# Weighted sums of two attention groups in a row, behind both groups' scores, in a fused convolution, scan, attention and expert kernel

## The chip, the cores and the metric

The kernel runs on one core of a Trainium2 chip. The metric is the device time of one execution in microseconds (us). Engines are called by the profile's names: PE (TensorE; PEld are its weight loads), DVE (VectorE), ACT (ScalarE), POOL (GpSimd), SP (SyncE, which issues almost all transfers).

## The reference, cut to what matters

For a batch of four images of 128 channels and 64 x 64 pixels, in float32:

```python
x = x + conv_layer(group_norm(x))      # layer 0: depthwise conv, norms, and a
                                       # state-space scan with 16 states per channel
t = to_tokens(x)                       # 4096 tokens of 128 channels per image
q, k, v = split(ln(t) @ W_qkv + b_qkv) # 4 heads of 32 channels
s = einsum('bhnd,bhmd->bhnm', q, k) / sqrt(128)
t = t + (softmax(s) @ v) @ W_proj + b_proj
p = softmax(ln(t) @ router_w)          # 8 experts, the best two weighted
t = t + sum over experts of p[e] * (ln(t) @ expert_w[e] + expert_b[e])
out = from_tokens(t)
```

The change touches the attention: scores, their exponential, and the sum of the values weighted by it. The softmax is not shifted by the row's maximum; each value tile has 32 columns of ones beside its 32 value columns, so that the weighted sum gives numerator and denominator together.

## The kernel before, in words

**Blocks and slots.** An image is cut into 8 blocks of 512 tokens. The scan of a block takes 2 x 16 units (two channel halves, 16 states), and the attention of an image takes 256 groups: 4 pairs of query blocks (1024 queries) x 4 heads x 16 groups, where one group is STEP = 2 key tiles of 128 keys. One loop (L966 to L997) writes out the program for all of it, one slot after the other. A slot takes one scan unit (image b) and one attention group (image b-1, once the last block of that image is closed), so the attention of one image runs beside the scan of the next. There are 1024 units and 1024 groups; the first image's scan has no attention beside it, and the last image's attention has no scan beside it. "Shared stretch" below is the time in which a slot has both, "alone" the time in which it has the attention only.

**One slot, in order of emission:**
1. the scores of group s (`attention`, L761): two tiles `sc`, 128 keys x 1024 queries, two matmuls each with f32r operands (L785), and for each an exponential on ACT into `pT` (L790);
2. one stage of lane Y (convolution, norms, inputs of the scan);
3. `y`: an identity matmul that adds the last unit's product `hc` to the block's result;
4. one scan unit (`scan`, L644): `da` on ACT (L648), two broadcast transfers `bb` and `cc`, on DVE the product `h` (L660), the scan (L663) and `hc` (L670), and on ACT a copy of the last column to `state` (L668);
5. the weighted sums `av` of group s-1 (`weighted`, L796): four matmuls, each two instructions, with 64-column weights; two 64-column halves of the array work side by side;
6. one stage of lane X: `closed` (L683: projection, norm, and the queries, keys and values of a finished block, stored to DRAM), `divided` (L818: transpose and normalise a head's sums), `finished` (L827: output projection, norm, router, 8 expert stages, result). An expert stage is one `ps_X` matmul and four multiply-adds `acc` on DVE (L899).

**What fixes the order.** Every PE instruction passes through `queued` (L434), which ties it to the one before, so PE runs exactly the order of emission. On the other engines a scheduler places the instructions: `da`, the scan and its transfers are placed up to three units ahead, as their tiles have three buffers; exponentials follow their scores. SP issues in one order too: a store that waits for its data holds up the loads behind it, among them `ks` (keys, L774, one per four groups).

**Buffers.** The scores have two PSUM tiles (`ps_sc`, L461), which one group fills; the scores of the next group wait until ACT has read them. `pT` has four buffers, that is two groups. The sums `av`, the scan's result `y`, and the work tiles `ps_X` and `ps_Y` have one PSUM tile each; lane X's next matmul waits until DVE or ACT has read the last `ps_X`. After a head's 16 groups DVE copies `av` to `avs` (L809), and the head's `divided` stage, put at the front of lane X, transposes it.

Of the kernel before, what the change touches and what calls it, by code (L numbers as in the profile page):

```python
# [9 lines left out]
F32 = mybir.dt.float32  # L10
# [7 lines left out]
P = 128  # L18
C = 128
EPS = 1e-5  # L20
BLK = 512
NT = BLK // P
# [3 lines left out]
DH = 32  # L26
NH = 4
NE = 8
# [8 lines left out]
def conv_mamba_attn_moe_kernel(ctx: ExitStack, tc: tile.TileContext, t: dict):  # L37
    nc = tc.nc
    x, out = t["x"], t["out"]
    B, _, L = x.shape  # L40
# [68 lines left out]
    with (  # L109
# [20 lines left out]
        for i, (w, bias) in enumerate(((wqn, bqn), (wkn, bkn))):  # L130
            for h in range(NH):
# [9 lines left out]
                k = NH * i + h  # L141
# [318 lines left out]
    mix, att, side = pool("mix"), pool("att"), pool("side")  # L460
# [4 lines left out]
    def work(lane, shape=None):  # L465
        return ps_work.tile(shape or [P, BLK], F32, tag=f"work{lane}", name=f"ps_{lane}")

    def tmp(lane, name, shape=None):
        return side.tile(shape or [P, BLK], F32, tag=f"tmp{lane}", name=name, bufs=3)
# [206 lines left out]
        nc.gpsimd.tensor_mul(zs, xin, zs)  # L676
        gated[b, i, p] = zs

    vst = [side.tile([P, NH, NT, 2 * DH], F32, name=f"vst{k}") for k in range(2)]
    for w in vst:  # L680
        nc.gpsimd.memset(w[:, :, :, DH:], 1.0)

    def closed(b, i):  # L683

        if i == 0:
            kqv[b] = (
                dram.tile([2, P, L], F32, name="kd"), dram.tile([2, P, L], F32, name="qd"),
                dram.tile([NH, NB, P, NT * 2 * DH], F32, name="vd"),
                dram.tile([P, NTILE * C], F32, name="td"),
            )  # L690
        kd, qd, vd, td = kqv[b]
        s = slice(i * BLK, (i + 1) * BLK)
        ps = work("X")
        mm(ps.rearrange("p (r w) -> p r w", w=IMG), ident, y0_rows(b, i), True, False)
        mm(ps, skipI, xn_of[b, i][:, 3:], False, False)
        mm(ps, wout[:, 0, :], gated.pop((b, i, 0)), False, False)
        mm(ps, wout[:, 1, :], gated.pop((b, i, 1)), False, True)
        cm = tmp("X", "cm")
        nc.scalar.copy(cm, ps)
        yield  # L700
        xt = normalised("X", by_tile(transposed("X", by_tile(cm))))
        yield
        yield
        ps = transposed("X", xt)
        f = tmp("X", "f")
        nc.scalar.activation(f, ps, AF.Identity, bias=lnb, scale=lnw)
        xs = x_block(b, i, "xr")
        yield
        ps = work("X", [P, NT, C])
        for j in range(NT):  # L710
            r = slice(j * P, (j + 1) * P)
            summed(ps[:, j, :], [(f[:, r], projT), (xs[:, r], ident)])
        tt = side.tile([P, NT, C], F32, name="tt", bufs=2)
        nc.vector.tensor_add(tt, ps, projb[:, None, :].to_broadcast([P, NT, C]))
        nc.sync.dma_start(out=tsave[b][:, s], in_=tt.rearrange("p j c -> p (j c)"))
        xt = normalised("X", tt)

        nc.gpsimd.tensor_add(tt, tt, crow[:, None, :].to_broadcast([P, NT, C]))
        nc.sync.dma_start(out=td[:, s], in_=tt.rearrange("p j c -> p (j c)"))
        yield  # L720
        yield
        ps = transposed("X", xt)
        xa = side.tile([P, BLK], F32, name="xa", bufs=1)
        nc.scalar.copy(xa, ps)
        yield
        for d, w, bias in ((kd, wkn, bkn), (qd, wqn, bqn)):
            ps = work("X")
            mm(ps, w, xa)
            full = tmp("X", "full")
            nc.scalar.activation(full, ps, AF.Identity, bias=bias)  # L730
            hi = side.tile([P, BLK], F32R, name="hi")
            nc.scalar.activation(hi, ps, AF.Identity, bias=bias)
            lo = side.tile([P, BLK], F32R, name="lo")
            nc.vector.tensor_sub(lo, full, hi.bitcast(F32))
            nc.sync.dma_start(out=d[0][:, s], in_=hi.bitcast(F32))
            nc.sync.dma_start(out=d[1][:, s], in_=lo.bitcast(F32))
            yield
        ps = work("X", [P, NT, NH, DH])
        for j in range(NT):
            mm(ps[:, j].rearrange("p h d -> p (h d)"), xa[:, j * P : (j + 1) * P], wv)  # L740
        w = vst[i % 2]
        nc.vector.tensor_copy(w[:, :, :, 0:DH], ps.rearrange("p j h d -> p h j d"))
        nc.sync.dma_start(
            out=vd[:, i].rearrange("h p q -> p h q"), in_=w.rearrange("p h j d -> p h (j d)")
        )
        yield

# [48 lines left out]
    def weighted(group):  # L796
        b, qp, h, k0, pTs, ao = group
        if k0 == 0:
            sums[0] = ps_av.tile([P, BLK], F32, name="av")
        av = sums[0]  # L800
        for k, (v, pT) in enumerate(pTs):
            for u in range(2):
                mm(
                    av[64 * u : 64 * u + 2 * DH, :], v, pT[:, u, :],
                    k0 + k == 0, k0 + k == NTILE - 1,
                )
        if k0 + STEP == NTILE:
            avs = att.tile([P, BLK], F32, name="avs", bufs=2)
            nc.vector.tensor_copy(avs, av)  # L809
            lanes["X"].appendleft((("div", b, qp, h), divided(h, avs, ao), []))  # L810
            if h == NH - 1:
                for u in range(2):
                    qb = 2 * qp + u
                    lanes["X"].append(
                        (("out", b, qb), finished(b, qb, ao[:, u]), [("div", b, qp, h)])
                    )
# [10 lines left out]
    def finished(b, qb, ao):  # L827
# [5 lines left out]
        ps = transposed("X", ao.rearrange("p j h d -> p j (h d)"))  # L833
# [3 lines left out]
        ps = work("X", [P, NT, C])  # L837
# [4 lines left out]
        yield  # L842
        yield
        ps = transposed("X", xt)
        xf = side.tile([P, BLK], F32, name="xf")
        nc.scalar.copy(xf, ps)
        yield
        ps = work("X", [P, NT, NE])
# [41 lines left out]
        for j in range(NT):  # L890
            for u in range(2):
                ps = work("X", [P, NE // 2, C])
# [4 lines left out]
                for e in range(NE // 2):  # L897
                    k = NE // 2 * u + e
# [6 lines left out]
        ps = work("X")  # L905
        for j in range(NT):
            queued(nc.tensor.transpose(ps[0:NE, j * P : (j + 1) * P], pr[:, j, :], ident))
        prT = side.tile([NE, BLK], F32, name="prT")
        nc.scalar.copy(prT, ps[0:NE, :])
        yield  # L910
        ps = work("X")
# [9 lines left out]
    lanes, done, running = {"X": deque(), "Y": deque()}, set(), {}  # L921

    def advance(lane):

        while True:
            if lane not in running:
                if not lanes[lane] or not all(k in done for k in lanes[lane][0][2]):
                    return False
                running[lane] = lanes[lane].popleft()
            key, stages, _ = running[lane]  # L930
            try:
                next(stages)
                return True
            except StopIteration:
                done.add(key)
                del running[lane]
# [13 lines left out]
    for k in range(-2, len(blocks)):  # L950
        if 0 <= k:
            b, i = blocks[k]
            Y.append((("in", b, i, 1), inputs(b, i, 1), [("scan", *blocks[k - 1], 1)] if k else []))
        if k + 2 < len(blocks):
            b, i = blocks[k + 2]
# [3 lines left out]
        if 0 <= k + 1 < len(blocks):  # L959
            b, i = blocks[k + 1]  # L960
# [4 lines left out]
            ))  # L965

    units = iter([(b, i, p, n) for b, i in blocks for p in range(2) for n in range(NST)])
    term, waiting, groups, image = None, None, None, 0
    unit = next(units)
    while unit or term or waiting or image < B or lanes["X"] or running:  # L970
        if groups is None and image < B and ("closed", image, NB - 1) in done:
            groups = attention(image)
            image += 1
        group = next(groups, None) if groups is not None else None
        if groups is not None and group is None:
            groups = None
        advance("Y")
        if term:
            b, i, p, n, hc, y = term
            mm(y, ident, hc, n == 0, n == NST - 1)  # L980
            if n == NST - 1:
                scanned(b, i, p, y)
                done.add(("scan", b, i, p))
                if p == 1:
                    lanes["X"].appendleft((("closed", b, i), closed(b, i), []))
            term = None
        if unit:
            b, i, p, n = unit
            until(("in", b, i, p))
            if n == 0:  # L990
                y = ps_y.tile([P, BLK], F32, name="y")
            term = b, i, p, n, scan(b, i, p, n), y
            unit = next(units, None)
        if waiting:
            weighted(waiting)
        waiting = group
        advance("X")  # L997
    main.close()

    with tc.If(nc.values_load(general[0:1, 0:1]) > 0):
# [4 lines left out]
        with tc.For_i(0, B, 1) as b:  # L1007
            t_tok = whole.tile([P, NTILE, C], F32, name="t_tok")
            xa = whole.tile([P, L], F32, tag="xcm", name="xa")
            nc.sync.dma_start(  # L1010
                out=t_tok.rearrange("p k c -> p (k c)"),
                in_=tsave[bass.ds(b, 1)].rearrange("o p q -> (o p) q"),
            )
            with tc.tile_pool(name="ps_again", bufs=4, space=PSUM) as psum:
                for i in range(NB):
                    ps = anew(t_tok[:, NT * i : NT * (i + 1), :], psum)
# [86 lines left out]
```

## Time and profile before

| what | value |
|---|---|
| time, median of 3 runs | 6684.65 us (6683.0 to 6687.69) |
| profiled execution, its own time | 6685.48 us |
| its span, first to last instruction | 6683.4 us |
| mean granted PE clock | 0.924 |
| PE busy | 5909.8 us (88%) |
| DVE busy | 4012.6 us (60%) |
| ACT busy | 3703.8 us (55%) |
| `sc` matmuls | 4096 instructions, 1329.3 us |
| `av` matmuls | 8192 instructions, 2019.5 us |
| exponentials | 2048, 1020 ns each, 1985.6 us |
| first `sc`, last `y` | 1202.7 us, 5652.6 us |

The profiled execution took 0.8 us more than the median. Busy times of PE are modelled ends and overlap; start-to-start times of its instructions are exact. A bracket behind an instruction gives the idle time before it and what ended it. Four stretches are told apart below: before the first attention (to 1203 us), shared (to 5703 us), alone (to 6572 us) and the end.

### The profile page before, as it was taken

How to read it: one execution, taken by the hardware profiler on the slowest of the kernel's cores; microseconds unless marked ns; L12 is line 12 of the kernel's file. 1: busy time of each engine (PE TensorE's matmuls, PEld its weight loads, DVE VectorE, ACT ScalarE, POOL GpSimd, SP SyncE). 2: the span in 40 equal slices, each digit the busy share in tenths (PEclk: the TensorE clock that was granted, in tenths of full speed). 3: DMA queues.
4: the chain of work that ended last, by engine and by line, in shares of the span. 5: the costliest groups of instructions: out<-in, count | busy, mean ns of one | idle time of the engine just before them, and what ended most of it. 6: DMA issues, size and time to landing. Idle time of an engine off the chain costs nothing.

```text
span 6683.4 us, 69800 instructions
## 1 busy us (share of the span) xinstructions
PE 5909.8 (88%) x20282; PEld 2468.2 (37%) x20282; DVE 4012.6 (60%) x7806; ACT 3703.8 (55%) x5245; POOL 859.8 (13%) x895
## 2 busy tenths in 40 slices
PE   5777666899999898999989899999989899999996
PEld 2222222334344333434434343343434343444442
DVE  4788888666666575666757576666757575211122
ACT  2444434665565555566566565656556565555552
POOL 1212212111111111111111111111111110000000
PEclk7677767999999999999999999999999999999997
DMA  3454555555454654555555555445555455322220
GB/s 87 141 160 144 159 156 152 156 162 150 135 147 136 168 136 132 150 143 149 139 157 142 150 149 148 137 142 154 146 155 146 133 160 148 96 71 72 74 72 6
DMA packets 536343, 895.74 MB, mean 134 GB/s; under 512 B 100097, under 2 KB 183442, under 8 KB 535954
## 3 DMA queue, kind: packets, MB, share of 16 engines
q1 hardware_dynamic: 534786, 890.41, 47.0%
q8 instruction: 164, 2.69, 0.2%
q14 instruction: 225, 1.84, 0.1%
q10 hardware_dynamic: 1168, 0.80, 0.0%
HBM read 806.93 MB, written 83.89 MB: 133 GB/s over the span
## 4 chain that ended last, share of the span: by engine, by line
PE 54%; DVE 7%; DMA 3%; ACT 3%; issue 2%; POOL 1%; SPq 1%; DVEq 0%; ACTq 0%; POOLq 0%
PE av L444 21%; PE sc L444 11%; PE ps_X L444 9%; PE y L444 7%; PE ps_Y L444 4%; DMA bb<-bcd 2%; PE ps_X L474 1%; DVE h L663 1%; DVE xt L493 1%; DVE h L660 1%; DVE acc L899 1%; ACT pT L790 1%; DVE hc L670 1%; DMA ks<-kd 1%; PE ps_Y L474 1%
## 5 line engine op out<-in xcount | busy, mean ns | idle before, releaser
L790 ACT ACTIVATE pT<-sc 128x1024 f32<-128x1024 f32 x2048 | 1985.6, 1020 | 1033.1 <-PE sc L444 1031.1
L444 PE MATMUL av<-pT,v 128*64 128x512 f32 x8192 | 2019.5, 614 | 0.0
L444 PE MATMUL y<-hc,ident 128*128 128x512 f32 x2048 | 1244.8, 694 | 283.4 <-DVE hc L670 281.4
L444 PE MATMUL sc<-qs,ks 128*128 128x512 f32 x4096 | 1329.3, 446 | 123.0 <-DMA ks<-kd 55.4
L663 DVE TENSOR_TENSOR_SCAN h<-da,state,h 128x512 f32<-128x512 f32 x896 | 1194.0, 1333 | 58.3 <-DVE h L660 2.3
L444 PEld LDWEIGHTS av<-pT,v 128*64 128x64 f32 x8192 | 504.9, 138 | 1312.9 <-issue 1256.6
L444 PEld LDWEIGHTS sc<-qs,ks 128*128 128x128 f32 x4096 | 724.5, 191 | 659.7 <-issue 331.4
L660 DVE TENSOR_TENSOR h<-bb,du 128x512 f32<-128x512 f32 x1024 | 731.7, 715 | 373.5 <-DMA bb<-bcd 359.0
L648 ACT ACTIVATE da<-delta,amat 128x512 f32<-128x512 f32 x1024 | 738.5, 723 | 159.4 <-DVE h L663 150.5
L670 DVE TENSOR_TENSOR hc<-cc,h 128x512 f32<-128x512 f32 x1024 | 753.7, 737 | 90.7 <-DMA cc<-bcd 33.6
L668 ACT COPY state<-h 128x1 f32<-128x1 f32 x896 | 171.4, 192 | 993.3 <-DVE h L663 990.9
L444 PEld LDWEIGHTS y<-hc,ident 128*128 128x128 f32 x2048 | 396.7, 213 | 663.9 <-DVE hc L670 479.4
L899 DVE SCALAR_TENSOR_TENSOR acc<-ps_X,pr,acc 128x128 f32<-128x128 f32 x1024 | 356.1, 348 | 382.7 <-PE ps_X L444 361.5
L444 PE MATMUL ps_X<-w_ew,xf 128*128 128x512 f32 x512 | 302.2, 673 | 46.1 <-DVE acc L899 45.4
L809 DVE COPY avs<-av 128x512 f32<-128x512 f32 x64 | 44.1, 689 | 453.6 <-PE av L444 453.5
L489 POOL TENSOR_SCALAR rsX<-mvX 128x4 f32<-128x4 f32 x96 | 42.2, 440 | 1932.9 <-DVE mvX L487 1932.9
L444 PE MATMUL ps_Y<-y,taps 128*128 128x512 f32 x576 | 281.3, 627 | 3.7 <-ACT y L554 1.7
L444 PE MATMUL ps_Y<-xn,inxc 64*128 64x512 f32 x512 | 249.0, 628 | 2.5 <-DVE delta L630 1.6
L634 POOL TENSOR_TENSOR lost<-e,lost 128x512 f32<-128x512 f32 x64 | 99.7, 1558 | 1099.7 <-DVE lost L633 1091.8
L493 DVE TENSOR_SCALAR xt<-ps_Y,mvY,rsY 128x128 f32<-128x128 f32 x384 | 132.3, 404 | 171.4 <-POOL rsY L490 171.4
L489 POOL TENSOR_SCALAR rsY<-mvY 128x4 f32<-128x4 f32 x96 | 44.0, 458 | 1294.4 <-DVE mvY L487 1292.0
L676 POOL TENSOR_TENSOR zs<-xin,zs 128x512 f32<-128x512 f32 x64 | 106.2, 1660 | 722.6 <-DVE xin L675 722.5
(207 smaller groups left out, 4613.9 us busy)
## 6 DMA issues: line engine op xcount, KB each, us to landing
bb<-bcd SPq DMA_DIRECT2D x2048, 128.0 KB, 3.4
cc<-bcd SPq DMA_DIRECT2D x2048, 128.0 KB, 3.5
ks<-kd SPq DMA_DIRECT2D x1024, 128.0 KB, 3.4
v<-vd SPq DMA_DIRECT2D x256, 256.0 KB, 3.9
qs<-qd SPq DMA_DIRECT2D x256, 128.0 KB, 3.4
vd<-vst SPq DMA_DIRECT2D x32, 512.0 KB, 3.2
xg<-in_x SPq DMA_DIRECT2D x32, 256.0 KB, 4.1
gn<-in_x SPq DMA_DIRECT2D x32, 256.0 KB, 3.9
```

What stands on the lines that cost most here:

```text
L444: queued(nc.tensor.matmul(out, lhsT=lhsT, rhs=rhs, start=start, stop=stop))
L474: queued(nc.tensor.transpose(ps[:, j * P : (j + 1) * P], src[:, j, :], ident))
L493: nc.vector.tensor_scalar(xt[:, j, :], src[:, j, :], mv[:, j, 0:1], rs[:, j : j + 1], ALU.subtract, ALU.mult)
L634: nc.gpsimd.tensor_sub(lost, e, lost)
L648: nc.scalar.activation(da, delta, AF.Exp, scale=amat[:, n : n + 1])
L660: nc.vector.tensor_mul(h, bb, du)
L663: nc.vector.tensor_tensor_scan(out=h, data0=da, data1=h, initial=0.0 if i == 0 else state[:, p, n : n + 1], op0=ALU.mult, op1=ALU.add,)
L668: nc.scalar.copy(state[:, p, n : n + 1], h[:, BLK - 1 : BLK])
L670: nc.vector.tensor_mul(hc, cc, h)
L676: nc.gpsimd.tensor_mul(zs, xin, zs)
L790: nc.scalar.activation(pT, sc, AF.Exp, scale=ATT_SCALE)
L899: nc.vector.scalar_tensor_tensor(acc[:, j, :], ps[:, e, :], pr[:, j, k : k + 1], acc[:, j, :], ALU.mult, ALU.add,)
```

## The change

The loop no longer takes the weighted sums of group s-1 in slot s. It collects two groups, and when both have their scores, it writes out the weighted sums of both in a row, behind lane X's stage. Over two slots PE's order was

    sc0 Y y av X | sc1 Y y av X

and becomes

    sc0 Y y X | sc1 Y y X av0 av1

The groups' number per head (16) is even, so a pair never spans two heads. Beside that, five tiles lose buffers or move to the shared `tmpX` ring of three: `vst` (2 buffers to 1), `tt` (2 to 1), `xa`, `xf`, `prT`. The PSUM pools and the buffers of `pT`, `ks` and `v` stay.

```diff
-    vst = [side.tile([P, NH, NT, 2 * DH], F32, name=f"vst{k}") for k in range(2)]
-    for w in vst:
-        nc.gpsimd.memset(w[:, :, :, DH:], 1.0)
+    vst = side.tile([P, NH, NT, 2 * DH], F32, name="vst")
+    nc.gpsimd.memset(vst[:, :, :, DH:], 1.0)
...
-        tt = side.tile([P, NT, C], F32, name="tt", bufs=2)
+        tt = side.tile([P, NT, C], F32, name="tt")
...
-        xa = side.tile([P, BLK], F32, name="xa", bufs=1)
+        xa = tmp("X", "xa")
...
-        xf = side.tile([P, BLK], F32, name="xf")
+        xf = tmp("X", "xf")
...
-        prT = side.tile([NE, BLK], F32, name="prT")
+        prT = tmp("X", "prT")[0:NE, :]
...
-    term, waiting, groups, image = None, None, None, 0
+    term, waiting, groups, image = None, [], None, 0
...
-        if waiting:
-            weighted(waiting)
-        waiting = group
         advance("X")
+        if group:
+            waiting.append(group)
+
+        if len(waiting) == 2 or (waiting and group is None):
+            for group in waiting:
+                weighted(group)
+            waiting = []
```

More of the change, by code (lines that the diff above doesn't have):

```diff
@@ L740, in closed @@
             mm(ps[:, j].rearrange("p h d -> p (h d)"), xa[:, j * P : (j + 1) * P], wv)
-        w = vst[i % 2]
-        nc.vector.tensor_copy(w[:, :, :, 0:DH], ps.rearrange("p j h d -> p h j d"))
+        nc.vector.tensor_copy(vst[:, :, :, 0:DH], ps.rearrange("p j h d -> p h j d"))
         nc.sync.dma_start(
-            out=vd[:, i].rearrange("h p q -> p h q"), in_=w.rearrange("p h j d -> p h (j d)")
+            out=vd[:, i].rearrange("h p q -> p h q"), in_=vst.rearrange("p h j d -> p h (j d)")
         )
@@ L967, in conv_mamba_attn_moe_kernel @@
     units = iter([(b, i, p, n) for b, i in blocks for p in range(2) for n in range(NST)])
-    term, waiting, groups, image = None, None, None, 0
+    term, waiting, groups, image = None, [], None, 0
     unit = next(units)
-    while unit or term or waiting or image < B or lanes["X"] or running:
+    while unit or term or waiting or groups or image < B or lanes["X"] or running:
         if groups is None and image < B and ("closed", image, NB - 1) in done:
```

## The prediction

> **What bounds the kernel now.** I read the busy time by stretch first, then the waits of the shared stretch, then PE's instructions in order of time, then the waits that remain. By stretch (columns: stretch, length, then PE, PEld, DVE, ACT, POOL busy with instruction counts, granted clock, DMA share, GB/s):
>
> ```profile
> 1203.00:5703.00 4500.00, 4169.06 (x14937) 1775.33 (x14937) 2889.97 (x5538) 2720.93 (x3866) 601.62 (x615) 0.97 0.53 147
> 5703.00:6572.00 869.00, 862.21 (x3548) 357.25 (x3547) 164.91 (x583) 511.78 (x550) 10.11 (x16) 1.00 0.24 69
> ```
>
> PE sets the pace: 93% busy in the shared stretch, 99% alone. But busy PE is not useful PE. PE's own timeline, four plain slots (start, length, instructions):
>
> ```profile
> 3010.73 1.20 PE L444 MATMUL sc<-qs,ks 128*128 128x512 f32 x4
> 3011.76 1.02 PE L444 MATMUL y<-hc,ident 128*128 128x512 f32 x2
> 3012.71 1.94 PE L444 MATMUL av<-pT,v 128*64 128x512 f32 x8
> 3014.58 1.20 PE L444 MATMUL sc<-qs,ks 128*128 128x512 f32 x4
> ```
>
> A slot is 3.85 us. In the single records two `y` instructions are 0.429 apart, an `av` instruction costs 0.2145 on average, an `sc` one 0.235. From these, `y` to `av` should take 0.86 and takes 0.95 (+0.09); eight `av` should take 1.72 and take 1.87 (+0.15); `sc` to `y` should take 0.94 and takes 1.04 (+0.10). So entering and leaving an `av` run costs **0.34 us**, in every slot.
>
> What waits are there in the shared stretch (waiting instruction, released by, us in total, times, longest):
>
> ```profile
> PE y L444 <- DVE hc L670: 91.5, 37, 5.2
> PE sc L444 <- DMA ks<-kd: 55.4, 17, 8.3
> PE ps_X L474 <- DVE avs L809: 52.2, 28, 3.6
> PE sc L444 <- ACT pT L790: 7.9, 21, 1.5
> ```
>
> The last line matters most: today scores hardly wait for the exponentials, because 1.87 us of `av` lie between one group's scores and the next. The change takes that cover out of every first half of a pair.
>
> **The change part by part.** All sums stand against the profiled execution, 6685.5 us, 0.8 above the median.
>
> *Fewer runs of `av`.* The order of PE's instructions in the changed program has 512 `av` runs instead of 1024. Alone: 128 runs less, charted below. Shared: 384 x 0.346 = 133, times 0.93 (the share in which PE is the pace; elsewhere another wait takes the gain over) = **-124**. A rule of the Trainium skill speaks against this: "TensorE: Matmul & The Clock Gate", Part 2, step-by-step, has PE pull weight loads ahead of matmuls in flight. By it the border would be nearly free and my sum some 168 us higher. Here the first weight load of `av` is not pulled ahead: it starts at 3012.71, with its matmul, 0.76 us after the load before it.
>
> *Head's end.* `divided` ran right behind the last `av` and waited for the copy `avs` (0.69 us). Now scores and `y` (1.04 + 0.86) lie between. Gone: the 52.2 above x 0.93 = **-48**; alone, 59.4 on the page less 52.2 = -7.
>
> *Lane X ahead of `av`.* X1 now runs before two `av` runs instead of directly before the next scores, so what hangs on X1 has 3.7 us more. The case where this pays, on PE and SP:
>
> ```profile
> 2583.67 1.12 PE L444 MATMUL ps_X<-xa,w_wqn 128*128 128x512 f32 x2
> 2590.82 2.04 PE L444 MATMUL sc<-qs,ks 128*128 128x512 f32 x4 [6.03 <-DMA ks<-kd]
> 2592.66 1.91 PE L444 MATMUL y<-hc,ident 128*128 128x512 f32 x2
> ```
>
> ```profile
> 2586.12 0.34 SPq L735 DMA_DIRECT2D qd<-hi  x1
> 2586.85 0.34 SPq L736 DMA_DIRECT2D qd<-lo  x1
> 2587.24 0.45 SPq L756 DMA_DIRECT2D ks<-kd  x1
> ```
>
> SP's queue is held by the store of the queries, which waits for X1's matmul, ACT and DVE; the keys behind it land 7.1 us after X1 begins. Charted with the new order from sc0 (2575.37) at 0, with the durations around it: X0 at 1.80, sc1 2.66 to 3.60, X1 at 4.46; ACT does sc1's exponentials to 6.3, then X1's two copies to 7.7, DVE the third to 8.4, the store is out at 8.8, the keys land 3.5 later (2587.24 to 2590.73). sc2 starts at 12.35 instead of 15.45: 3.1 less, 2.8 beyond the border. Twelve such waits of 5 to 6.3 us: -33. Twenty-one other waits ahead of an even group's scores could save 34 (each up to 2.07); half of it, 17. Together **-50**. The skill's clock rule (same page, Part 1: half speed after an idle window of 3.4 us) would add 12 x 1.7 = 20, as the wait falls to about 3 us. Not counted: `y` runs at half speed after the 6.03 wait (1.91 for 1.02), but at 2569.03 a wait of 2.92 was followed by `av` at 3.68 for 1.94 too.
>
> *Shared stretch, the price.* From sc0 to sc1 the distance shrinks by 1.87 of `av` plus 0.20 of border: 2.07. For every second slot I took from the single records how long before its start each PE stage had its inputs and buffers ready, and charged what 2.07 exceeds that by, the largest once per slot. In 214 to 229 of 384 slots something is late: scores behind exponentials 42, expert matmuls behind `acc` 43 (`ps_X` is one buffer), other stages of X and Y 63, `y` behind `hc` 103. Of the last, 26 slots wait newly (25 us); 35 wait already (77 us), mostly for `bb` behind a store held by X one slot earlier, which now comes sooner. They could as well gain 72. I take none of it: 42 + 43 + 63 + 25 = **+173**; bounds for `y` alone -72 to +103.
>
> *Alone.* No `y`, no Y, and lane X only sometimes. The slots now (PE and ACT):
>
> ```profile
> 5895.85 1.20 PE L444 MATMUL sc<-qs,ks 128*128 128x512 f32 x4
> 5896.68 1.94 ACT L790 ACTIVATE pT<-sc 128x1024 f32<-128x1024 f32 x2 [1.06 <-PE sc L444]
> 5896.98 1.94 PE L444 MATMUL av<-pT,v 128*64 128x512 f32 x8
> 5898.84 1.20 PE L444 MATMUL sc<-qs,ks 128*128 128x512 f32 x4
> ```
>
> 2.99 a slot, 5.99 a pair. New pair, from sc0 at 0: exponentials start at 0.83, end at 1.80 and 2.77; a score can follow 0.05 later (smallest distance in the records). PE reaches sc1 at 1.04, waits to 1.85 for the first tile and to 2.82 for the second, ends at 3.29; then 0.14 entry, 16 x 0.2145 = 3.43, 0.09 exit: 6.95, so +0.96. With an expert stage in both slots (3.86 each now): sc1's second tile still waits to 2.82; X1 waits for X0's multiply-adds, which end 2.67 after its matmul begins at 1.04 (now 5804.68 to 5807.35), so until 3.76; the pair ends at 8.28 for 7.72: +0.56. In the changed order's 128 pairs, between sc0 and sc1 stand: nothing in 57 (55 us), four transposes of 0.59 in 25 (same end 6.95 for 6.58: 9), a matmul of 0.86 in 38 (32 expert pairs 18, six at +0.1), others in 8. Sum 83, less 7 for the heads' ends: **+76**, borders included.
>
> *Free.* `vst`, `tt`, `xa`, `xf`, `prT`: each is next written many slots after its last reader (blocks come 32 slots apart, and in lane X's program order no ring tile comes round before its reader is done). If that cover failed, a DVE or ACT write would wait about one landing per block, 32 x 3.2 us (`vd<-vst` on the page) = 102. The sums and exponentials themselves are unchanged; `av1` needs an exponential that ends at 4.71 in the chart and is read at 5.15.
>
> Sum: -124 - 48 - 50 + 173 + 76 = +27: 6685.5 + 27 = **6712 us**.
>
> **Rivals.** (1) *Lane X's early start wins (faster)*: the held stores on SP go out 2 to 4 us sooner, so `bb`, `h` and `hc` come sooner too. Place: the 35 slots in which `y` waits today. Price: -72, and if half of the other 148 is covered by waits already there, -74 more: 6712 - 146 = 6566 at best, about 6620 at half. It decides if the shared stretch falls by more than 76, what the lone stretch loses. For it: those waits stand at fixed places in each block behind stores. Against: ACT, DVE and `ps_X` serve one slot at a time, and half the slots lose 2.07 of slack.
>
> (2) *`y` pays in full*: +77, and the short `ks` waits give nothing, +17: 6806. Against it the same fixed places.
>
> (3) *The terms cancel* (within 0.2%, 13 us, about what this kernel's measurement can tell): 6685.
>
> (4) *It doesn't do what it says*: the border is paid between av0 and av1 as well; 168 + 27 gives 6880. Nothing in the records shows a cost between `av` instructions on different `pT`, so almost nothing for it.
>
> **How the numbers follow.** Forecast, a small loss (6699 to 6760) 0.37; rival 1 0.32; rival 2 0.17; rival 3 0.13; rival 4 0.01. Slower 0.37 + 0.17 + 0.01 = 0.55, same 0.13, faster 0.32. Range 6600 to 6800: it holds rival 1 down to a little below its half and nearly all of rival 2; the likeliest sign's own range is 6699 to 6760.
>
> **What would show it.** Alone grows from 869 to about 945, and idle time of the `sc` weight loads behind ACT there well beyond 104 us; shared shrinks by about 50; PE's wait for `avs` near 0; waits for `ks` down by some 30; waits for `acc` and `hc` up. The issue-idle of `av` weight loads (1256.6 us on the page) must halve; if not, rival 4. I am wrong if the lone stretch doesn't grow (PE would not wait for the exponentials), or if `y`'s waits move by more than 70 either way.

## The result, and the profile after

The changed kernel takes 6802.1 us (median of 4 runs, 6789.12 to 6810.56), against 6685.0 for the kernel before on the same chip: ratio 1.0173, 95% interval 1.0156 to 1.0191. It is slower, as forecast, but by 117 us and not by 27, and 2 us beyond the range. The profiled execution is the lowest of the four, 6789.12 us with a span of 6787.2, so the stretches below add up to 104 and not to 117.

First the stretches of the changed kernel, shared and alone (columns as in the prediction: stretch, length, then PE, PEld, DVE, ACT, POOL busy with instruction counts, granted clock, DMA share, GB/s):

```profile
1201.00:5709.00 4508.00, 4115.75 (x14938) 1822.28 (x14939) 2906.28 (x5540) 2718.06 (x3866) 624.76 (x615) 0.97 0.54 147
5709.00:6674.00 965.00, 886.99 (x3543) 361.51 (x3541) 164.63 (x582) 505.45 (x550) 10.12 (x16) 1.00 0.22 62
```

From group to group in the records, the lone stretch grew from 868.8 to 965.7: **+97**. The shared stretch went from 4500.2 to 4507.5: **+7**, where I had expected -49. In the shared stretch PE's busy time fell by 53 and its idle time rose by 61; the second line shows PE idle for 78 of 965 us alone, where it had been idle for 7.

What the lone stretch now looks like, on PE and then on ACT (start, length, instructions, idle before and its releaser):

```profile
6002.00 1.10 PE L444 MATMUL ps_X<-w_ew,xf 128*128 128x512 f32 x2 [0.20 <-DVE acc L897]
6003.03 3.65 PE L444 MATMUL av<-pT,v 128*64 128x512 f32 x16
6006.61 1.20 PE L444 MATMUL sc<-qs,ks 128*128 128x512 f32 x4
6007.65 1.02 PE L444 MATMUL ps_X<-w_ew,xf 128*128 128x512 f32 x2
6008.52 0.73 PE L444 MATMUL sc<-qs,ks 128*128 128x512 f32 x2
6009.44 0.73 PE L444 MATMUL sc<-qs,ks 128*128 128x512 f32 x2 [0.18 <-ACT pT L788]
6010.36 0.60 PE L905 MATMUL ps_X<-ident,pr 128*8 128x128 f32 x4 [0.19 <-DVE acc L897]
```

```profile
6007.44 3.85 ACT L788 ACTIVATE pT<-sc 128x1024 f32<-128x1024 f32 x4 [4.52 <-PE sc L444]
```

The sixteen `av` run on in 3.65 us, eight pairs at 0.429 and the last one's own end: nothing is paid between the two groups. But the second group's scores are cut in two tiles of two, and the second waits. ACT says why: it works through four exponentials without a gap from 0.83 us after the first score, and has had 4.52 us of idleness before. Twice the scores and exponentials now fall together and then stand still together.

In the shared stretch, what PE waits for (us in total, times, longest):

```profile
PE y L444 <- DVE hc L670: 109.9, 50, 5.8
PE ps_X L444 <- DVE acc L897: 87.0, 45, 9.6
PE sc L444 <- ACT pT L788: 50.5, 124, 3.1
...
PE sc L444 <- DMA ks<-kd: 26.4, 10, 8.6
```

`avs` is down to 0.8 us and `ks` by 29, as worked out; `acc` (16.8 before), the exponentials (7.9) and `hc` took their place.

### The profile page after: what moved, and what is told of

Its sections match the earlier page's. It is cut to its first block, busy times and chain, and to the rows that moved or that the text cites. A ratio compares the mean times of both kernels' runs of the same rounds, so it can differ in the third digit from the quotient of the medians.

```text
span 6787.2 us, 69668 instructions
## 1 busy us (share of the span) xinstructions
PE 5878.5 (87%) x20282; PEld 2519.8 (37%) x20282; DVE 4028.5 (59%) x7806; ACT 3695.9 (54%) x5245; POOL 882.2 (13%) x894
## 5 line engine op out<-in xcount | busy, mean ns | idle before, releaser
L444 PE MATMUL av<-pT,v 128*64 128x512 f32 x8192 | 1913.9, 609 | 8.6 <-ACT pT L788 8.6
L444 PE MATMUL y<-hc,ident 128*128 128x512 f32 x2048 | 1222.9, 683 | 302.2 <-DVE hc L670 300.0
L444 PEld LDWEIGHTS sc<-qs,ks 128*128 128x128 f32 x4096 | 683.2, 189 | 951.3 <-issue 518.1
L444 PEld LDWEIGHTS av<-pT,v 128*64 128x64 f32 x8192 | 551.5, 139 | 1203.1 <-issue 1071.7
L444 PEld LDWEIGHTS ps_X<-w_ew,xf 128*128 128x128 f32 x512 | 93.8, 201 | 262.7 <-issue 175.9
```

Of the source, the lines that this page charges most:

```text
L444: queued(nc.tensor.matmul(out, lhsT=lhsT, rhs=rhs, start=start, stop=stop))
```

## The experiments

Theories, by the letters that the expectations use. **A**: the second group's scores wait for the first group's exponentials. **B**: lane X's stages follow too closely on `ps_X`, whose one buffer waits for the multiply-adds into `acc`. **C**: the shared stretch is paced by another chain (SP, transfers, the scan on DVE), so that what PE saves is taken back there, whichever wait shows it. **D**: the lost buffers cost. **Y**: `y` comes before its product `hc`. **S** (formed late): exponentials are late because they queue behind ACT's copy `state`, which waits for the scan.

Two measures are used. Ratios are against the kernel before on the same chip. Stretches come from one profile each, and profiles on different chips differ: e2 below has a ratio of 0.9998, and a shared stretch 14 us shorter than the first profile of before. So stretches on one chip are set against each other where that is to be had.

### Parts of the change alone

e1, one group at a time, lane X ahead of its weighted sum (against before):

```diff
+        advance("X")
         if waiting:
             weighted(waiting)
         waiting = group
-        advance("X")
```

> Only lane X's place changes: a slot is scores, Y, y, X, av of the group before; one group at a time, buffers as before. Theory A (the pair uncovers the second group's scores, and that alone spoils it): no pair, no uncovered scores; PE's wait for the copy of a head's sums (59 us before) goes to nearly 0 and part of the keys' waits (55 us) too, so 60 to 100 us faster, 6585 to 6625. Theory C (in the shared stretch a chain over SP, transfers and VectorE sets the end, and whatever PE gains there is taken back): shared stretch 4500 as before, 6675 to 6690.

Ratio 0.9828 (0.9815 to 0.9842), 6556.08 us: the fastest of the kernels here that do the whole work. Shared 4380.1, alone 865.5. The move of lane X, which the change brings along, is worth 1.7% by itself; the pairing loses it and more. What PE still waits for in e1's shared stretch:

```profile
PE y L444 <- DVE hc L670: 50.5, 29, 5.4
PE sc L444 <- DMA ks<-kd: 35.5, 13, 5.4
```

Before, these two were 91.5 and 55.4; the wait for `avs` is down from 52.2 to 4.9.

e2, the buffer edits alone (the first half of the change's diff, with before's loop):

> The five buffer edits alone (vst, tt, xa, xf, prT), with the loop of before. Theory A and C: no tile is written again before its readers are long done, 6678 to 6692. Theory D (the buffer edits are part of the loss): a wait of a few us per block, 30 to 100 us slower.

Ratio 0.9998 (0.9989 to 1.0007); shared 4486.4, alone 868.7. Theory D falls.

e3, pairs, but the second slot's lane X behind the two sums:

```diff
-        advance("X")
         if group:
             waiting.append(group)
...
             waiting = []
+        advance("X")
```

> The changed kernel with the second slot's lane X behind the two weighted sums instead of ahead of them. Theory A: the uncovered scores stay (110 us of wait in the shared stretch, 117 alone), the waits for the copy of the sums (about 60) and for the keys (about 55) come back: 6880 to 6920. Theory C: shared stretch as it is, about 6800.

6842.89 us in a single run, shared 4558.2, alone 972.5. Between the two groups' scores stands the same work as in the change; only the second stage of lane X has moved, from ahead of the two sums to directly ahead of the next scores. The shared stretch is 51 us longer than that of the change's pairs on the same chip (e4, below). PE's waits for `avs` are back at 23.2 us (0.8 in the changed kernel), those of `y` for `hc` are 132.3 (109.9).

e4, pairs only while scan terms run beside them, before's order alone:

```diff
+        if unit or term:
+            advance("X")
+            ...
+        else:
+            for old in waiting:
+                weighted(old)
+            waiting = [group] if group else []
+            advance("X")
```

> Pairs as long as the scan runs beside the attention, one group at a time (order of before) in the last image. Theory A: the lone stretch falls from 965 back to about 869, the shared one stays at about 4508: 6690 to 6715. Theory B (lane X's single work buffer is what the pair costs): only some 10 us of the lone stretch come back, about 6790.

Ratio 1.0024 (1.0015 to 1.0034): shared 4507.2, alone 868.8. So of the change's 1.73% the lone stretch holds about 1.5, all of it given back by the order alone. On this chip e1, e2 and e4 stand side by side: lane X ahead takes 4486 to 4380 (**-106**), and pairs on top of it take 4380 to 4507 (**+127**).

### One suspected wait taken away at a time

e5 (on e1) and e6 (on the changed kernel), exponentials cut short so that scores hardly wait for them:

```diff
-                        pT = att.tile([P, 2, BLK], F32, name="pT", bufs=4)
-                        nc.scalar.activation(pT, sc, AF.Exp, scale=ATT_SCALE)
+                        pT = pTf[turn[0] % 4]
+                        turn[0] += 1
+                        nc.scalar.activation(
+                            pT[:, :, 0:64], sc[:, :, 0:64], AF.Exp, scale=ATT_SCALE
+                        )
```

> Control: one group at a time, lane X ahead of av (the order of e1_x_first), and each exponential covers 128 of its 1024 columns (the other columns of pT keep ones written at the start), so the scores' buffers come free some 0.7 us sooner each. Theory A (the pair's loss is the second group's scores waiting for exponentials): scores hardly waited here, so the lone stretch stays at 866 and the shared one falls little, 4330 to 4380. Theory C (the shared stretch is set by SP, transfers and VectorE): the same.

> The changed kernel with the same short exponentials. Theory A: the second group's scores don't wait any more; the lone stretch falls from 965 to about 825 (866 less 128 x 0.34), the shared one from 4508 to below 4400. Theory B (what the pair costs in the shared stretch is lane X's single work buffer and the scan's products coming late): lone stretch the same 825 to 845, but the shared one still above 4430.

A single run each; an exponential covers 128 of its 1024 columns, and the other columns of `pT` keep ones. e5: 6524.98 us, shared 4347.0, alone 864.6. e6: 6606.29, shared 4427.3, alone 867.7. Alone, the stretch is 98 us shorter with the exponentials cut, which is as much as the pairs had lost. PE's timeline of e6 there:

```profile
5910.52 1.20 PE L444 MATMUL sc<-qs,ks 128*128 128x512 f32 x4
5911.56 0.60 PE L474 MATMUL ps_X<-ident,ao 128*128 128x128 f32 x4
5911.91 1.17 PE L444 MATMUL sc<-qs,ks 128*128 128x512 f32 x4
5912.92 1.07 PE L444 MATMUL ps_X<-w_wp,aT 128*128 128x128 f32 x8
5913.92 3.65 PE L444 MATMUL av<-pT,v 128*64 128x512 f32 x16
```

The second group's four scores run as one block, with nothing in brackets. A plain pair (no stage of lane X in it) falls from 7.07 to 5.88 us. Theory A is shown for the plain pairs. The 28 pairs with an expert stage in both slots don't move, 8.36 us with and without the cut, for there theory B holds as well; PE's longest wait in e6's lone stretch is the one for `acc`:

```profile
PE ps_X L444 <- DVE acc L905: 21.5, 28, 0.8
```

Such an expert pair takes 7.92 with one multiply-add alone (e7) and 7.35 with both cuts (e12). In the shared stretch the pair gains 80 and the single order 33.

e7, the changed kernel with one of four multiply-adds into `acc` per expert stage:

```diff
-                for e in range(NE // 2):
+                for e in range(1):
```

> The changed kernel with one multiply-add per expert stage instead of four (three of four experts' products are left out), so lane X's work buffer comes free about 1.0 us sooner. Theory B: PE's wait for it (98 us in the shared stretch) falls by most, the shared stretch from 4508 to 4420 or less. Theory A: 30 to 50 us, since scores wait on instead.

6697.4 us in a single run, shared 4460.0 (-47), alone 952.9 (-13). What PE waits for in its shared stretch:

```profile
PE y L444 <- DVE hc L670: 146.0, 68, 5.6
PE sc L444 <- ACT pT L788: 47.8, 115, 3.1
...
PE ps_X L444 <- DVE acc L897: 17.1, 11, 4.4
```

The wait for `acc` fell by 70 (87.0 to 17.1), and that for `hc` rose by 36. Half of what is taken away at one place comes back at the next.

e10 (on e1) and e11 (on the changed kernel), `y` one slot later:

```diff
-        if term:
-            b, i, p, n, hc, y = term
+        if len(terms) == 2 or (terms and not unit):
+            b, i, p, n, hc = terms.popleft()
...
+            terms.append((b, i, p, n, scan(b, i, p, n)))
```

> One group at a time, lane X ahead of av (e1_x_first, ratio 0.983, shared stretch 4380), and y takes the scan's product of two units ago instead of the last one. Theory Y (PE comes to y before the scan's product is there, 57 us of wait; a slot more of distance hides it): shared stretch 4320 to 4350, ratio 0.974 to 0.979. Theory C (the scan's chain over transfers and VectorE is itself behind at these places, so PE only waits later): 4370 to 4390, ratio 0.982 to 0.985.

> The changed kernel (pairs) with the same later y. Theory Y: PE's wait for the scan's product, 122 us there, falls below 40, the shared stretch from 4507 to 4400 to 4440. Theory C: the wait only moves to the next scores or lane stage, 4490 to 4510.

e10: ratio 0.9852 (0.9836 to 0.9869), no better than e1; shared 4361.3, but from a start some 34 us later, so the time did not follow. e11: 6769.63 in a single run, shared 4455.4 (-52), alone 965.7. Again the waits of e11 tell where the rest went:

```profile
PE ps_X L444 <- DVE acc L897: 102.4, 43, 8.0
PE sc L444 <- ACT pT L788: 71.9, 139, 3.3
PE sc L444 <- DMA ks<-kd: 39.9, 18, 5.4
```

`hc` has left the list (109.9 before the edit); `acc` has 15 more, the exponentials 21, the keys 14.

### All of them together

e12 (pairs) and e13 (the single order of e1): short exponentials, one multiply-add and the later `y`.

> The changed kernel with all three waits taken away at once: short exponentials (128 of 1024 columns, the rest of pT is ones), one multiply-add per expert stage instead of four, later y. If these three are what the pair costs, the saved border shows in full against e13: lone stretch 44 below it (about 820), shared stretch 90 to 130 below it. Theory C: lone stretch so, but the shared stretch no better than e13's, or above it.

> Control for e12: one group at a time, lane X ahead of av, with the same three cuts. Lone stretch 865; shared stretch 4280 to 4340 (4347 with short exponentials alone, less what the later y and the missing multiply-adds give).

A single run each: 6465.35 and 6465.17 us. e12: shared 4315.3, alone 835.3. e13: shared 4286.0, alone 864.6. Alone the pair is now ahead by 29, of the 44 (128 x 0.346) that its border is worth; an expert pair, with 7.35 us where the order before took 7.71, has it in full, a plain one, 5.88 for 5.99, only a third: even the short exponential (0.83 after the first score, then 0.28 long) ends after PE is back at the scores, which start 1.16 us after the first ones where 1.04 was possible. In the shared stretch the pair is still 29 behind, where its saved border should put it some 124 ahead. ACT's own waits in e12's shared stretch:

```profile
ACT state L668 <- DVE h L663: 962.6, 470, 6.5
ACT da L648 <- DVE h L663: 151.8, 72, 6.3
```

Of 54 second slots in which scores still waited (61 us), the exponentials were late in all, and in 39 of them ACT had stood before `state`. So theory S: `state` on ACT holds the exponentials up.

e14 (on e1), e15 (on the changed kernel), e16 and e17 (on e12 and e13) put that copy on DVE:

```diff
-            nc.scalar.copy(state[:, p, n : n + 1], h[:, BLK - 1 : BLK])
+            nc.vector.tensor_copy(state[:, p, n : n + 1], h[:, BLK - 1 : BLK])
```

> One group at a time, lane X ahead of av (e1_x_first: ratio 0.983, shared 4380), with the copy of the scan's last column on VectorE behind the scan instead of on ScalarE. Theory S (ScalarE stands before this copy until the scan is done, and exponentials behind it come late): few scores are late here, so 10 to 40 us less in the shared stretch. Theory C (the scan's chain on VectorE and the transfers sets the stretch): 896 more VectorE instructions of about 0.1 to 0.2 us make it 0 to 100 us longer.

> The changed kernel (pairs, shared 4508, alone 965) with the same move. Theory S: the 54 late exponentials go, some 40 to 60 us less in the shared stretch; alone unchanged. Theory C: not shorter.

> Pairs with the three cuts of e12_all_pair (short exponentials, one multiply-add per expert stage, later y: shared 4315) and the copy on VectorE. Theory S: the border shows at last, shared stretch 50 to 130 below e17's. Theory C: the pair still isn't ahead of e17 by more than 20.

> Control for e16: single groups, lane X ahead, the same four cuts (e13_all_single without the copy's move: 4286). Theory S: 4260 to 4286. Theory C: 4290 to 4380.

e14: ratio 0.9852 (0.9835 to 0.9868), shared 4377.0. e15: 6794.54, shared 4506.7. e16: 6468.01, shared 4313.2. e17: 6474.63, shared 4289.7. Nothing moves by more than the profiles of two chips differ. The same wait of ACT in e16:

```profile
ACT da L648 <- DVE h L663: 1103.3, 526, 6.5
```

It has only gone from `state` to `da`, the next instruction, whose buffer the scan must free: 962.6 + 151.8 = 1114.4 before, 1103.3 now. Theory S falls. ACT's stream is tied to the scan on DVE at two places, and freeing one is worth nothing.

### Another spacing

e9, to give the pair its cover back: in each round of two slots all of lanes Y and X and both `y` are spread around the two groups' scores, and both sums are written at the end; the single order of e1 alone.

```diff
+            advance("X")
+        for _ in range(2 if beside else 1):
+            advance("Y")
             if term:
...
+            second = next(groups) if group else None
+            advance("X")
+            if group:
+                weighted(group)
+                weighted(second)
```

> Pairs whose second scores stand far from the first: beside the scan two slots are scores, X, Y, y, Y, y, scores, X, av, av; alone, one group at a time with lane X ahead of av. Theory A: scores find their buffers free (two y of 0.86 and a stage of X between), the border is saved 384 times, so 60 to 120 us faster than lane X's move alone: ratio 0.965 to 0.974. Theory C: nothing beyond lane X's move, ratio about 0.983; if two y in a row wait for the scan's products, above that.

Ratio 1.0207 (1.019 to 1.0224): shared 4603.4, alone 865.5. What theory A gave for it is missed by a wide margin. PE's waits in e9's shared stretch:

```profile
PE y L444 <- DVE hc L670: 190.7, 81, 5.8
PE av L444 <- ACT pT L788: 66.6, 50, 3.6
PE ps_X L444 <- DVE xt L493: 64.9, 15, 5.0
```

The scores' waits are gone from the head of the list; 81 us more of `y` and 58 more of `av` than in the changed kernel stand there. Two terms close together ask for two products in quick succession, where the change's order asks for one per slot.

### Where PE's time goes, kernel by kernel

In the records of single matmuls I added up the distances from each start to the next in the shared stretch, by what they lead to. The five sums make up the stretch exactly: *av* (into, within and out of `av`, up to the second scores instruction), *sc* (the other two scores), *y*, *X*, *Y*.

| kernel | av | sc | y | X | Y | shared |
|---|---|---|---|---|---|---|
| e1, single | 2113 | 374 | 601 | 807 | 485 | 4380 |
| e4, pairs (same chip) | 2034 | 411 | 674 | 884 | 505 | 4507 |
| changed kernel | 2029 | 413 | 673 | 885 | 508 | 4508 |
| e6, pairs, short exponentials | 1990 | 374 | 693 | 882 | 489 | 4427 |
| e7, pairs, one multiply-add | 2024 | 409 | 721 | 799 | 507 | 4460 |
| e11, pairs, later `y` | 2073 | 418 | 544 | 913 | 507 | 4455 |
| e12, pairs, all three | 2035 | 380 | 553 | 830 | 516 | 4315 |
| e13, single, all three | 2112 | 364 | 540 | 771 | 499 | 4286 |

e1 to e4 is the price of pairing term by term: -78 + 36 + 73 + 77 + 20, 127 as rounded sums go. And the rows below show C at work: e7 takes 86 off X and gives 48 back at `y`; e11 takes 129 off `y` and gives 28 back at X and 45 in the *av* sum, at the first scores.

These sums hold more than work and waiting: PE's clock differs too. The shared stretches of e1 and e4 (columns as above, the granted clock behind the counts of POOL):

```profile
1201.00:5581.00 4380.00, 4143.51 (x14937) 1789.22 (x14935) 2881.81 (x5540) 2723.73 (x3868) 628.80 (x615) 0.98 0.53 151
1198.00:5705.00 4507.00, 4128.30 (x14934) 1822.69 (x14935) 2911.14 (x5538) 2717.54 (x3866) 624.27 (x615) 0.97 0.51 147
```

In the records of these traces the granted clock is either 1 or 0.5. Pieces at 0.5 (3.4 us long or a multiple of that) add up to 292 us in e2's shared stretch, 164 in e1's and 301 in e4's. They follow idleness of PE: in the 3.5 us before a fall e4's PE has stood still for 2.3 us in the median, before any other moment for none. Half of PE's busy time in these pieces is my estimate of what they cost: 120 us in e2, 72 in e1, 126 in e4, and 49 in e13 against 91 in e12. By that estimate some 48 of the 106 that lane X's move gains, and some 54 of the 127 that pairs cost on top of it, are PE running slowly after a wait. No run changes the clock by itself, and the waits that follow would take a part of it back, so these shares are not shown by an experiment. The mean clock of the whole execution repeats: 0.933 to 0.935 in all five runs of e1, 0.923 to 0.928 in all ten of e4.

## Why the prediction was wrong

The sign was right, and the waits that the prediction names are those that appeared; the sum was 90 short of the median (6712 for 6802): 56 in the shared stretch (+7 for -49), 21 alone (+97 for +76), and 13 that the profiled execution lies below the median. To judge the shared stretch by the prediction's own terms I set each distance between two PE starts against a short one (the 5% point) between the same instructions at full clock, and put the rest down to what the second one had waited for. From e2 (before's order) to e4 (pairs), on one chip, in us:

| term of the shared stretch | predicted | e2 to e4 |
|---|---|---|
| fewer runs of `av` | -124 | -135 |
| head's end, `avs` | -48 | -50 |
| lane X ahead: keys and values ahead of scores | -50 | -65 |
| scores behind exponentials | 42 | 87 |
| their restart (the last section) | 0 | 16 |
| expert matmuls behind `acc` | 43 | 74 |
| other stages of X and Y | 63 | 48 |
| `y` behind `hc` | 25 | 27 |
| sums behind their own exponentials | 0 | 15 |
| half clock, other waits | 0 | 4 |
| sum | -49 | 21 |

Against the 25% point the first row comes to -147 and the restart to 24; no other row moves by more than 6. The first profiles of before and after give the same picture, with 95 for the scores, 74 for `acc` and 25 for `y`, and a sum of 7.

- **Fewer runs of `av`, -124: right.** No border lies between the two groups, and with short exponentials the *av* sum of the pairs (e6) lies 116 below that of the single order on the same chip (e5, 2105). Rival 4 is refuted. The test that I gave for it was a bad one: the issue-idle of `av`'s weight loads fell only from 1256.6 to 1071.7 and not to half, since most of that idleness is not border.
- **Head's end -48, lane X ahead -50: right in the whole change.** Alone (e1 against e2, on one chip) lane X's move gives -106 for the -98, but this nearness is partly luck: beside `avs` and the keys it also shortens `y`'s waits by 42, which was rival 1's place and not counted, and the time at half clock; and it gives some of that back at other waits. The pairs then take `y`'s gain away again, 69 from e1 to e4, and the time at half clock with it; the 20 us at the clock that the prediction mentions without counting them did not come (120 in e2, 126 in e4).
- **Shared stretch, the price +173: the step that failed.** Its four terms measured 236, and two that the prediction put at nothing took 31 more. Worst sized was *scores behind exponentials*: 42 predicted, 87 measured, and 16 on top for scores that restart after a wait. *Expert matmuls behind `acc`* come next, 74 for 43; sums that wait for their own exponentials are the other 15. `y` was right, 27 for 25.
- **Why it failed.** I charged each slot from the slack of the old trace. But PE was late in that trace too, and a slack measured behind a late PE holds only as long as PE stays as late. And I charged the largest wait of a slot once, as if a PE that has waited for one thing had waited for all. That these two made the terms too small is argued and not shown; e7 and e11 do show that PE meets the next wait for about half of what one wait gives back. From e13 to e12, with three waits cut, the pairs' 77 less in *av* is still outweighed by 16 in *sc*, 59 in X, 17 in Y and 13 in `y`; an estimated 39 of these 105 are half clock.
- **Alone, +76: right in mechanism, +97 in size.** The chart's plain pair was 6.95 and is 7.07, the expert pair 8.28 and 8.36. The 0.12 is mostly the restart: scores that have waited start with a step of 0.335 instead of 0.235, and the second tile's end sets the pair. Over 128 pairs that is at most 15 of the 21; the rest I haven't placed. (The chart's 1.80 for the first exponential's end should be 1.85, as one takes 1.02; nothing hangs on it, since the second tile sets the pair.) The weight loads of the scores waited 104 us behind ACT alone and now 181, as the prediction asked:

```profile
PEld sc L444 <- ACT pT L788: 180.7, 241, 1.1
```

- **Buffers at nothing: right** (e2).
- **Rivals.** Rival 1 (lane X's early start wins) is what e1 shows, 1.7%, with `y`'s wait for `hc` at 50.5 for 91.5; that the earlier stores on SP bring this about was not tested. With pairs on top (e4) that wait is back at 110.7. (Half of its 146 would have been 6639 and not 6620.) Rival 2 (`y` pays in full, 6806) came nearest in time, by luck: neither the 77 that it charged more at `y` nor the 17 at the keys was paid. Rival 3 falls with the interval. The sign that I gave for being wrong, `y`'s waits moving by more than 70, did not appear: they went from 91.5 to 109.9.

**What stays open.** In e12 and e16 the scores still wait about 60 us for exponentials that are late behind `state` or `da`, which wait for the scan; that much of theory C is seen in the trace, though no run made the scan itself earlier. Which transfer or DVE step makes the scan late there was not tried. The 59 us of X in e12 are by estimate some 12 us of half clock and for the rest many small waits (`acc`, `xt`, `ao`, `f`), none over 28; they have no single cause that the runs show. What the clock alone costs was not tried either.

## What to carry to other kernels

Count a saved switch on the bounding engine together with the spacing that it takes away: two bursts of scores and two of sums need the engine between them (here ACT, 2 x 0.97 us per group) to do in half the time what it did in the whole. Here that cost 97 us alone, the saved borders already taken off; in the shared stretch the lost spacing cost some 250 us (127 + 124) against the 124 of the switch, at the exponentials, `acc`, `hc` and the clock together. When a change has two parts, try each alone: lane X ahead of the sums was worth 1.7% and was hidden behind the pairing. Where several chains stand close behind the bounding engine, count on getting back only a part of a wait that you take away: here about half, in e7 and e11.

## What the runs showed of the hardware

- Leaving one shape of matmul for another cost PE 0.346 us per `av` run in and out, and nothing between 16 `av` in a row. The Trainium skill's "TensorEngine Tiling (Array Packing)", Key Properties, says that a change of the tiling mode drains TensorE; the records fit that and put a price on it, though they don't show the drain itself. The other matmul on 64 columns, `ps_X<-xin,wbc`, pays the same in the kernel before: 0.327 us into it from scores (0.232 to other work of 128 x 128), 0.523 out of it (0.429 for 512 columns that stay in their shape).
- A PE that has waited in the middle of a run of scores does not go on at the old step: the first distance after the wait is 0.335 us, for 0.235, as it is after `av`. Cutting one run of scores in two thus costs 0.10 beside the wait (this is the restart above).
- In the changed kernel's lone stretch ACT takes up a group's first exponential 0.83 us after the first score's start in the median (0.80 to 1.22), and PE goes on no sooner than 0.05 us after an exponential's end. With these two numbers and the durations the lone pair could be charted to within 0.12 us.
- A wait shorter than the 3.4 us that the prediction reckoned with was met by half clock: in the kernel before, PE stood still for 2.92 us up to 2569.03, the clock was 0.5 from 2568.0 to 2574.8, and the eight `av` behind it took 3.68 us for 1.94.
